# Block 0's first transposed tokens move into the tile of the forms, and its first residual runs its readings before the sums, the biases and LayerNorm's small operations

## The chip, the cores and the metric

The kernel runs on one core of a Trainium2 chip. A core has TensorE (matrix products from SBUF into PSUM), VectorE, ScalarE and GpSimd, each with a queue of its own that runs in order, and DMA queues, most of whose transfers SyncE issues. Engines wait for each other through semaphores alone. The metric is the device time of one execution in microseconds (us), the median of several runs.

In the profile PE is TensorE's matmuls, PEld its weight loads, DVE is VectorE, ACT is ScalarE, POOL is GpSimd and SP is SyncE. L701 is line 701 of the kernel before.

## What is computed

The input x has two sequences of 2048 tokens of 512 values, and each sequence has a condition vector. The condition gives six vectors (shift, scale and gate for each of two halves), and each half is a LayerNorm, a modulation and a two-layer network with a gated residual:

```python
emb = silu(t) @ ada_w + ada_b
shift_msa, scale_msa, gate_msa, shift_mlp, scale_mlp, gate_mlp = split(emb, 6)
norm  = ln(x) * (1 + scale_msa) + shift_msa
h     = gelu_exact(norm @ ssm_w1 + ssm_b1)            # 512 -> 512
x     = x + gate_msa * (h @ ssm_w2 + ssm_b2)          # 512 -> 512
norm2 = ln(x) * (1 + scale_mlp) + shift_mlp
hf    = gelu_tanh(norm2 @ ff_w1 + ff_b1)              # 512 -> 1024
x     = x + gate_mlp * (hf @ ff_w2 + ff_b2)           # 1024 -> 512
```

All values are float32.

## The kernel before

**Tiles and names.** The 4096 tokens are eight blocks of 512, each in an SBUF tile x of 128 partitions and four slots c of 512 values. Most large tiles come from one pool of eight buffers (`big`): brows, the x blocks, the weights ada_0 to ada_5 of the condition, the transposed tokens nT and the hidden values hA, hClo and hChi. A new tile takes a buffer that has been released, and its first write waits until the last reader of the old tile is done. The tile `forms`, 16 parts in all, is a constant. From block 1 on it holds sums of transposed tokens; in block 0 its first eight parts hold the hidden values hA (`hA_0`), and its other eight hold nothing that early.

**Products.** A layer is not one matrix product. Operands and results are cut in two by two, and seven products P1 to P7 are made where eight would be needed. The price is sums of operands before (three new operands per side, made by `sums_of_first` and `sums_of_second`: s0, s1, then one quarter changed in place, then s2) and sums of results after. Each product of 512 by 512 is a group of eight matmuls of 256 columns. The results of several products add up in one PSUM tile: P1, P6, P7 and P4 share the tile y, P5 and P3 the tile v, and P2 has x. After each product VectorE reads the tile (`after`), and the next product into the same tile waits for that reading. The products of block 0's and block 1's first layers and of their first residual run in the order `FIRST`, which is P1, P2, P5, P6, P7, P3, P4. P3 of a residual needs s2 of the hidden values, P5 and P6 need s0 and s1, P7 the quarter that is changed in place.

**The order is written by hand.** `hook(hooks, places, ops)` hangs operations behind products. After product P's matmuls and its reading have been issued, the operations hooked to P are issued, each to the queue of its engine. So where a hook stands decides what an engine does before what.

**The stage around the change.** For block 0 the start runs so: LayerNorm of block 0; the first halves of the modulation vectors of groups 0 and 1 (`modulation`, matmuls L279 with the weights ada_0 and ada_1); the transposes by TensorE (L898); the second halves of the same modulation; then `modulate` (L596 on ScalarE for k = 0 and 2, L598 on VectorE for k = 1 and 3), which writes nT; the sums nS of nT; the first layer (`First(0, ...)`, tiles py_hA, px_hA, pv_hA). Behind its products are hooked the rows of the gate, the folding of the gate into w2 (`fold2`: 0 to 3 are products on VectorE, 4 to 7 the four sums of w2 on GpSimd), the gated bias b2 that is added to x's slots on GpSimd (`gb2`, four operations L713, one for each slot), the first two statistics of block 1 and the modulation of group 3.

Then follows block 0's first residual (`residual("oA_0", ...)`, readings at L701). Behind its products are hooked the rest of the sums of the hidden values (`hA_sums`, tile hSA), the other two statistics of block 1, its LayerNorm scales (`scales`), its normals (`normal`, x times rstd plus nmr, L553 on ScalarE or L557 elsewhere), the modulation of group 4, the transposes of block 1 (`turned`), the first statistics of block 0's second LayerNorm, and the first three of the four sums of the weights fw1 (`fw1_sums`, GpSimd, tile fw_s; the third changes fw1 itself).

`scales` has two forms. Both begin on GpSimd with ve (L502) and the power r (L504). By default six more small operations run on GpSimd (L515 to L520); with `on_dve=True` four run on VectorE (L510 to L513).

**Loads.** SyncE issues the loads in the order of the program: x_0, ada_0 and ada_1 by halves, w1 by halves, ada_2, w2, b2, x_1, ada_3, ada_4, fw1, and, after the first modulation, ada_5, fw2 and rows of the second gate's bias.

From block 1 on the first layer of the second half is made of 26 products (`products`, L800) instead.

Of the kernel before, what the change touches and what calls it, by code (L numbers as in the profile page):

```python
# [140 lines left out]
def kernel(  # L141
# [16 lines left out]
    nc = tc.nc  # L158
# [3 lines left out]
    KD = D // P  # L162
    KH = H // P
    C = 4
# [29 lines left out]
    def big_tile(name):  # L194
        return big.tile([P, KD, D], F32, tag="big", name=name)
# [71 lines left out]
    def modulation(g0, part, half=None):  # L267


        g = g0 + part  # L270
        if not half:
            pada[g] = ps_g.tile([P, D], F32, tag="x", name=f"pada_{g}")
            mods[g0, part] = const.tile([P, KD, B], F32, tag=f"mod_{g0}_{part}", name=f"mod_{g0}_{part}")
        n = slice(0, KD) if half is None else slice(half * KD // 2, (half + 1) * KD // 2)
        pa = pada[g][:, n.start * G : n.stop * G]
        w = ada[g].rearrange("p k (n m q) -> p k m n q", n=KD, q=G)
        for k in range(KD):
            for m in range(P // G):
                nc.tensor.matmul(  # L279
                    pa[m * G : (m + 1) * G, :],  # L280
                    silu[:, k, :],
                    w[:, k, m, n],
                    start=(k == 0),
                    stop=(k == KD - 1),
                    tile_position=(0, m * G),
                    skip_group_check=True,
                )
        turned = pada[g][:, P + n.start * G : P + n.stop * G]
        bias = colsT[:, R_ADA + g * KD : R_ADA + (g + 1) * KD][:, n]

        def finish():
            nc.vector.transpose(turned, pa)
            to = mods[g0, part][:, n]
            by_n = turned.rearrange("p (n q) -> p n q", q=G)
            nc.vector.tensor_tensor(
                to, by_n[:, :, :B], bias.unsqueeze(2).to_broadcast([P, n.stop - n.start, B]), ALU.add
            )

        if half is not None:
            return finish  # L300
        finish()
# [106 lines left out]
    def weight_of_first(name, w_sb):  # L408

        K, M = w_sb.shape[1], w_sb.shape[2]  # L410
        tile_s = const.tile([P, 3, K // 2, M // 2], F32, tag=f"{name}_s", name=f"{name}_s")
        s = thirds(tile_s)
        lo, hi = w_sb[:, : K // 2, :], w_sb[:, K // 2 :, :]
        q = quarters(lo, hi, slice(0, M // 2), slice(M // 2, M))
        return first_operands(q, s), sums_of_first(q, s, nc.gpsimd), tile_s
# [58 lines left out]
    def hook(hooks, places, ops):  # L474

        for n, op in enumerate(ops):
            hooks.setdefault(places[min(n, len(places) - 1)], []).append(op)


    class Norm:  # L480
# [64 lines left out]
        def normal(self, c, eng=None, on_pe=False):  # L545

            if c == 0:
                self.nT = big_tile(f"nT{self.name}")
                self.xn = self.blocks().rearrange("p m k c q -> p m (k c q)") if on_pe else self.nT
            t = self.xn[:, c, :]  # L550
            x_c = xs[self.i][:, c, :]
            if eng is None:
                nc.scalar.activation(  # L553
                    t, x_c, AF.Identity, bias=self.nmr[:, c : c + 1], scale=self.rstd[:, c : c + 1]
                )
            else:
                eng.tensor_scalar(  # L557
                    t, x_c, self.rstd[:, c : c + 1], self.nmr[:, c : c + 1], ALU.mult, ALU.add
                )
# [127 lines left out]
    def residual(name, i, hops, wops, kdim, hooks, last=False, order=ORDER):  # L687

        xt = xs[i]
        F = D // 2  # L690
        q = {
            "11": xt[:, 0:2, :F],
            "12": xt[:, 0:2, F:],
            "21": xt[:, 2:4, :F],
            "22": xt[:, 2:4, F:],
        }
        dest = {"P1": "11", "P2": "11", "P6": "12", "P5": "22", "P7": "22", "P3": "12", "P4": "21"}

        def after(p, ps, js):
            d = q[dest[p]][:, js]  # L700
            nc.vector.tensor_tensor(d, ps[BANK[p]][:, js], d, ALU.add)  # L701
            if last and p in ("P7", "P4"):
                s = slice(2 + js.start, 2 + js.stop)
                f = slice(F, D) if p == "P7" else slice(0, F)
                nc.sync.dma_start(out=out_blk[i][:, s, f], in_=xt[:, s, f])

        parted = ("P1", "P6", "P7", "P4") if last else ()
        group(name, kdim, hops, lambda p, j, k: wops[p][:, k, :], after, hooks, parted, order)

    def biases(i, gb):  # L710

        return [
            lambda c=c: nc.gpsimd.tensor_tensor(xs[i][:, c, :], xs[i][:, c, :], gb, ALU.add)  # L713
            for c in range(C)
        ]
# [9 lines left out]

    forms = const.tile([P, 16, C, HT // C], F32, tag="forms", name="forms")

    hA_0 = forms[:, :8].rearrange("p n a r -> p (n a r)").rearrange("p (k t) -> p k t", k=KD)

    def sums_of_registers(program, reg, engs):  # L730

# [112 lines left out]
    n1 = {0: Norm(0, 1), 1: Norm(1, 1)}  # L844
# [22 lines left out]
    st = n1[0].stats()  # L867
# [59 lines left out]
    def fold2(lo, hi):  # L927
        return [lambda k=k: found["w2"][1][k]() for k in range(lo, hi)]
# [14 lines left out]
    hooks = {}  # L943
# [3 lines left out]
    st = n1[1].stats()  # L947
    hook(hooks, ("P6",), [rows_of_ssm_gate])
    gb2 = biases(0, b2_bc)
    hook(hooks, ("P3",), [ssm_gate, gb2_0] + gb2[:2] + fold2(0, 2))  # L950
    hook(hooks, ("P7",), fold2(2, 6) + gb2[2:] + fold2(6, 7))
    hook(hooks, ("P7", "P4"), st[:2])
    hook(hooks, ("P7",), [lambda: modulation(3, 0)])
    hA[0] = First(0, n1[0].ops, hooks, ("P1", "P2", "P5", "P6", "P3", "P7", "P4"), hA_0)
# [2 lines left out]
    hA_sums = hA[0].summed(nc.vector)  # L957
    run(hA_sums[:2])
    hooks = {}
    hook(hooks, ("P1",), hA_sums[2:3] + st[2:] + [n1[1].scales] + fold2(7, 8))  # L960
    hook(hooks, ("P2",), hA_sums[3:] + [lambda c=c: n1[1].normal(c, on_pe=True) for c in range(C)])
    hook(hooks, ("P6",), [lambda: modulation(3, 1)])
    hook(hooks, ("P3", "P3", "P4"), n1[1].turned())
    n2 = {0: Norm(0, 2)}
    st = n2[0].stats()
    hook(hooks, ("P3",), st[:2])
    fw1_ops, fw1_sums, fw1_s = weight_of_first("fw1", fw1_sb)
    hook(hooks, ("P2",), fw1_sums[:1])
    hook(hooks, ("P5", "P4"), fw1_sums[1:3])
    residual("oA_0", 0, hA[0], w2_ops, KD // 2, hooks, order=FIRST)  # L970

    def ff_gate():
# [12 lines left out]
    hooks = {}  # L985
# [15 lines left out]
    hA_sums = hA[1].summed(nc.vector)  # L1001
    run(hA_sums[:2])
    n1[2] = Norm(2, 1)
    st = n1[2].stats()
    hooks = {}
# [15 lines left out]
    hooks = {}  # L1021
# [26 lines left out]
    hooks = {}  # L1048
# [10 lines left out]
    hooks = {}  # L1059
# [6 lines left out]
    hooks = {}  # L1066
# [11 lines left out]
    for i in range(1, NBLK):  # L1078
        nxt, nx2, last = i + 1 < NBLK, i + 2 < NBLK, i + 1 == NBLK
        hC = Second(i)  # L1080
        hooks = {}
# [19 lines left out]
        hooks = {}  # L1101
# [16 lines left out]
        hooks = {}  # L1118
# [58 lines left out]
        hooks = {}  # L1177
# [52 lines left out]
```

## Time and profile before

| | us |
|---|---|
| median of 3 runs | 599.33 (598.78 to 599.54) |
| the profiled execution | 598.88 |
| its span, first to last instruction | 597.0 |

The profiled execution's own time is the one that its rows add up to; 1.9 us of it lie around the span.

The granted clock of TensorE is 1.00 in every stretch of this execution, so a matmul costs the same at each place: eight matmuls of 256 columns start 1.73 us after the eight before, where nothing is waited for.

The busy time of the engines by stretches of ten microseconds (us, from the profile's windows):

| stretch | DVE | ACT | POOL | DMA GB/s |
|---|---|---|---|---|
| 0 to 10 | 4.56 | 2.54 | 3.66 | 276 |
| 10 to 20 | 8.34 | 3.53 | 4.98 | 398 |
| 20 to 30 | 9.30 | 1.96 | 5.25 | 412 |
| 30 to 40 | 9.14 | 1.06 | 8.85 | 404 |
| 40 to 50 | 7.46 | 5.53 | 7.91 | 144 |
| 50 to 60 | 8.77 | 5.29 | 9.18 | 8 |
| 60 to 70 | 9.51 | 3.16 | 2.22 | 127 |
| 70 to 80 | 9.07 | 5.57 | 9.34 | 7 |
| 80 to 90 | 8.52 | 3.28 | 8.12 | 99 |

How to read it: the loads run at full speed until 40 us. VectorE is the fullest of the four in the stretch of the change. A stretched instruction (one that took longer because of another) counts as busy for its whole length.

The waits that the profile lists for TensorE's matmuls are few. In each line come the instruction that waited, what it waited for, the total in us, how often, and the longest:

```profile
PE idle L862 <- POOL ident masks.py:199: 1.3, 1, 1.3
PE py_oA L459 <- DVE x L701: 1.2, 1, 1.2
PE py_hA L459 <- ACT nT L596: 0.5, 1, 0.5
PE pt L898 <- ACT blocks L553: 0.2, 1, 0.2
```

The first belongs to the warm-up at the very start. The second is in block 0's first residual, the third at the first group of block 0's first layer.

### The profile page before, as it was taken

The numbers are of one execution on the slowest core, as the hardware profiler recorded it, in microseconds if no ns is written. First come the engines' busy times: TensorE is split into PE (matmuls) and PEld (weight loads), VectorE is DVE, ScalarE is ACT, GpSimd is POOL, SyncE is SP. The second block draws the span as 40 slices with busy tenths as digits, with TensorE's granted clock in tenths as the row PEclk, the third lists the DMA queues.
The fourth block names the chain that finished last, engine by engine and source line by source line (L and its number), as shares of the span: only waits on it lengthen the run. The fifth ranks groups of instructions, "written<-read, shape, count | busy, mean of one in ns | idle before, by whom it ended". The sixth has DMA issues, their size and how long they took to land.

```text
span 597.0 us, 8378 instructions
## 1 busy us (share of the span) xinstructions
PE 590.3 (99%) x2911; PEld 510.1 (85%) x2911; DVE 374.4 (63%) x646; ACT 219.7 (37%) x365; POOL 397.1 (67%) x467
## 2 busy tenths in 40 slices
PE   8999999999999999999999999999999999999997
PEld 4778888888888888888888888888888888888886
DVE  5978998897654375555754458653665246467642
ACT  2234347305432363233721356232553235212420
POOL 2698489999843995549968499966974596440200
PEclk9999999999999999999999999999999999999999
DMA  9990322300224003350042601321020300022001
GB/s 312 411 372 4 86 71 78 101 35 36 71 71 121 22 0 94 148 146 3 13 146 61 210 13 41 102 71 71 0 63 9 107 36 1 1 59 83 0 1 70
DMA packets 25065, 49.86 MB, mean 84 GB/s; under 512 B 4498, under 2 KB 8126, under 8 KB 24128
## 3 DMA queue, kind: packets, MB, share of 16 engines
q1 hardware_dynamic: 21984, 45.11, 22.7%
q10 hardware_dynamic: 3040, 4.22, 2.8%
q8 instruction: 23, 0.38, 0.3%
q14 instruction: 18, 0.15, 0.1%
HBM read 26.25 MB, written 8.39 MB: 58 GB/s over the span
## 4 chain that ended last, share of the span: by engine, by line
PE 96%; DVE 2%; issue 0%; ACT 0%; POOL 0%; POOLq 0%
PE py_oC L459 19%; PE px_hC L800 10%; PE pv_oC L459 9%; PE py_oA L459 9%; PE py_hA L459 9%; PE py_hC L800 8%; PE pv_hC L800 8%; PE pv_hA L459 5%; PE px_oC L459 5%; PE pv_oA L459 4%; PE py_hC L459 2%; PE px_hA L459 2%; PE px_oA L459 2%; PE pv_hC L459 1%; PE idle L862 1%; PE px_hC L459 1%
## 5 line engine op out<-in xcount | busy, mean ns | idle before, releaser
L713 POOL TENSOR_TENSOR x<-x,gb 128x512 f32<-128x512 f32 x64 | 80.3, 1286 | 8.7 <-ACT forms L670 4.7
L596 ACT ACTIVATE nT<-nT,mod,mod 128x512 f32<-128x512 f32 x54 | 39.6, 803 | 104.8 <-DMA nT<-blocks 98.0
L553 ACT ACTIVATE nT<-x,nmr,rstd 128x512 f32<-128x512 f32 x56 | 42.4, 803 | 52.6 <-POOL nmr L520 36.8
L502 POOL TENSOR_SCALAR ve<-mv 128x4 f32<-128x4 f32 x15 | 3.5, 233 | 82.2 <-DVE mv L494 81.9
L459 PE MATMUL py_oC<-fw,hClo 128*128 128x256 f32 x256 | 57.9, 379 | 0.0
L459 PEld LDWEIGHTS py_oC<-fw,hClo 128*128 128x128 f32 x256 | 48.6, 190 | 6.6
L701 DVE TENSOR_TENSOR x<-py_oC,x 128x512 f32<-128x512 f32 (+1 forms) x36 | 22.6, 629 | 42.6 <-PE py_oC L459 42.6
L493 DVE BATCH_NORM_STATS2 st<-x 128x6 f32<-128x512 f32 x64 | 43.4, 678 | 5.2 <-DMA x<-in_x_dram 5.0
L379 POOL TENSOR_TENSOR hSC<-hClo,hChi 128x512 f32<-128x512 f32 (+1 forms) x17 | 20.1, 1188 | 39.6 <-ACT hChi L795 29.2
L800 PE MATMUL py_hC<-forms,fw 128*128 128x256 f32 x168 | 40.8, 379 | 0.0
L817 DVE TENSOR_TENSOR hClo<-hClo,py_hC 128x512 f32<-128x512 f32 x42 | 28.4, 681 | 16.9 <-ACT hClo L814 10.3
L564 DVE STREAM_TRANSPOSE blocks<-nT 128x512 f32<-128x512 f32 x56 | 37.8, 693 | 1.5 <-ACT nT L553 1.1
L738 POOL TENSOR_TENSOR forms<-forms 128x256 f32<-128x256 f32 x48 | 35.6, 742 | 2.8
L800 PEld LDWEIGHTS py_hC<-forms,fw 128*128 128x128 f32 x168 | 31.8, 190 | 4.4
L817 DVE TENSOR_TENSOR hChi<-hChi,pv_hC 128x512 f32<-128x512 f32 x35 | 23.3, 683 | 17.1 <-PE pv_hC L800 17.1
L701 DVE TENSOR_TENSOR x<-py_oA,x 128x512 f32<-128x512 f32 x32 | 22.0, 688 | 19.2 <-PE py_oA L459 18.7
L459 PE MATMUL py_hA<-nT,w 128*128 128x256 f32 x128 | 30.4, 381 | 0.5 <-ACT nT L596 0.5
L795 ACT ACTIVATE hClo<-hClo,colsT 128x256 f32<-128x256 f32 x56 | 25.4, 500 | 10.8 <-DVE hClo L817 10.7
L459 PE MATMUL py_oC<-fw_s,hSC 128*128 128x256 f32 x128 | 28.9, 379 | 0.0
L459 PE MATMUL pv_oC<-fw,hSC 128*128 128x256 f32 x128 | 28.9, 379 | 0.0
L459 PE MATMUL px_oC<-fw,hChi 128*128 128x256 f32 x128 | 28.9, 379 | 0.0
L459 PE MATMUL pv_oC<-fw_s,hSC 128*128 128x256 f32 x128 | 28.9, 379 | 0.0
(227 smaller groups left out, 1428.4 us busy)
## 6 DMA issues: line engine op xcount, KB each, us to landing
nT<-blocks SPq DMA_DIRECT2D x168, 64.0 KB
out_dram<-x SPq DMA_DIRECT2D x15, 512.0 KB
x<-in_x_dram SPq DMA_DIRECT2D x7, 1024.0 KB
fw<-in_L_cond_ff_w_dram SPq DMA_DIRECT2D x3, 2048.0 KB
ada<-in_L_cond_ada_w_dram SPq DMA_DIRECT2D x4, 1024.0 KB
nT<-blocks ACTq DMA_DIRECT2D x56, 64.0 KB
ada<-in_L_cond_ada_w_dram SPq DMA_DIRECT2D x4, 512.0 KB
w<-in_L_cond_ssm_w_dram SPq DMA_DIRECT2D x2, 1024.0 KB
```

Source lines behind the costliest of these rows:

```text
L379: eng.tensor_tensor(out[:, r], a[:, r], b[:, r], f)
L459: nc.tensor.matmul(ps[b][j * apart][:, j, :], lhs(p, j, k), rhs(p, j, k), start=(fresh and j * (not apart) == 0 and k == 0), stop=(p in (" ...
L493: nc.vector.bn_stats(st, xs[self.i][:, c, :])
L553: nc.scalar.activation(t, x_c, AF.Identity, bias=self.nmr[:, c : c + 1], scale=self.rstd[:, c : c + 1])
L564: nc.vector.transpose(self.bl[:, :, :, c, :].rearrange("p m k q -> p k m q"), self.nT[:, c, :].rearrange("p (k m q) -> p k m q", k=KD, m=C),)
L596: nc.scalar.activation(dst, src, AF.Identity, bias=shift, scale=scale)
L701: nc.vector.tensor_tensor(d, ps[BANK[p]][:, js], d, ALU.add)
L713: lambda c=c: nc.gpsimd.tensor_tensor(xs[i][:, c, :], xs[i][:, c, :], gb, ALU.add)
L738: eng.tensor_tensor(reg[d], reg[a], reg[b], ALU.add if f == "+" else ALU.subtract)
L795: nc.scalar.activation(h, h, AF.Gelu_apprx_tanh, bias=fb1T[:, m : m + 1])
L800: nc.tensor.matmul(ps[b][:, j, :], fa[ra][:, j * P : (j + 1) * P], fb[rb].rearrange("p a (c q) -> p c a q", q=Q), start=(fresh and j == 0) ...
L817: nc.vector.tensor_tensor(dest(d), dest(d), ps[b], op)
```

## The change

1. nT of block 0's first LayerNorm no longer takes a buffer of the pool; it is the second half of `forms`. The later tiles of the pool take other buffers than before.
2. In block 0's first residual the third new operand of the hidden values (`hA_sums[3:]`) and block 1's scales and normals are hooked to P6, so that the readings of P2, P5 and P6 come before them in VectorE's queue.
3. The scales of block 1 are made on VectorE (after ve and r on GpSimd): four small operations more on VectorE, six fewer on GpSimd. The normal of slot 3 is made by VectorE in place of ScalarE.
4. The bias of slots 2 and 3 (`gb2[2:]`) moves from block 0's first layer to P7 of the residual. In GpSimd's queue the sums of w2 close up. Then come ve, r, the first sum of fw1, the two biases, and the second and third sum of fw1. Since P7's reading writes the same slots of x before, the biases now follow that reading, and P4's reading follows the biases.
5. The first sums of fw1 are hooked to P6, P3 and P4.

No other queue changes its order; SyncE's is the same.

```diff
         def normal(self, c, eng=None, on_pe=False):

             if c == 0:
-                self.nT = big_tile(f"nT{self.name}")
+                self.nT = nT_0 if self.name == "1_0" else big_tile(f"nT{self.name}")
...
-    hA_0 = forms[:, :8].rearrange("p n a r -> p (n a r)").rearrange("p (k t) -> p k t", k=KD)
+    hA_0, nT_0 = [
+        forms[:, n : n + 8].rearrange("p n a r -> p (n a r)").rearrange("p (k t) -> p k t", k=KD)
+        for n in (0, 8)
+    ]
...
     hook(hooks, ("P3",), [ssm_gate, gb2_0] + gb2[:2] + fold2(0, 2))
-    hook(hooks, ("P7",), fold2(2, 6) + gb2[2:] + fold2(6, 7))
+    hook(hooks, ("P7",), fold2(2, 7))
...
-    hook(hooks, ("P1",), hA_sums[2:3] + st[2:] + [n1[1].scales] + fold2(7, 8))
-    hook(hooks, ("P2",), hA_sums[3:] + [lambda c=c: n1[1].normal(c, on_pe=True) for c in range(C)])
-    hook(hooks, ("P6",), [lambda: modulation(3, 1)])
+    hook(hooks, ("P1",), hA_sums[2:3] + st[2:] + fold2(7, 8))
+    hook(hooks, ("P6",), [lambda: n1[1].scales(on_dve=True)] + hA_sums[3:] + [lambda: modulation(3, 1)])
+    hook(hooks, ("P6",), [lambda c=c: n1[1].normal(c, nc.vector if c == 3 else None, on_pe=True) for c in range(C)])
     hook(hooks, ("P3", "P3", "P4"), n1[1].turned())
...
-    hook(hooks, ("P2",), fw1_sums[:1])
-    hook(hooks, ("P5", "P4"), fw1_sums[1:3])
+    hook(hooks, ("P6",), fw1_sums[:1])
+    hook(hooks, ("P7",), gb2[2:])
+    hook(hooks, ("P3", "P4"), fw1_sums[1:3])
     residual("oA_0", 0, hA[0], w2_ops, KD // 2, hooks, order=FIRST)
```

## The prediction

> **What bounds the kernel.** I read the page first, then the chain of waits, then the timelines of TensorE, VectorE and GpSimd between 10 and 85 us, where every instruction that the change touches stands.
>
> ```profile
> PE 590.3 (99%) x2911; PEld 510.1 (85%) x2911; DVE 374.4 (63%) x646; ACT 219.7 (37%) x365; POOL 397.1 (67%) x467
> PE 96%; DVE 2%; issue 0%; ACT 0%; POOL 0%; POOLq 0%
> ```
>
> TensorE is the bound: 96% of the chain that ended last is its own work. Only the start of a group of eight matmuls can move. Groups follow each other every 1.73 us from 84 to 545 us, so what is won or lost before 84 us stays to the end. The one large hole in that stretch is here:
>
> ```profile
> 36.73 1.08 PE L279 MATMUL pada<-ada,silu 128*32 128x128 f32 x32
> 39.03 1.97 PE L459 MATMUL py_oA<-w,forms 128*128 128x256 f32 x8 [1.22 <-DVE x L701]
> ```
>
> P7 of block 0's second product could start at 37.65 (the last matmul of the modulation starts at 37.54) and starts at 39.03. It adds into the PSUM tile of P6, so it waits for VectorE's reading of P6, which is late because VectorE is busy without a gap from 25 to 39.3 us:
>
> ```profile
> 36.33 0.18 DVE L494 BATCH_NORM_AGGREGATE mv<-st 128x2 f32<-128x6 f32 x1
> 36.43 0.66 DVE L701 TENSOR_TENSOR x<-px_oA,x 128x512 f32<-128x512 f32 x1
> 37.00 0.68 DVE L379 TENSOR_TENSOR hSA<-forms,hSA 128x512 f32<-128x512 f32 x1
> 37.60 0.68 DVE L701 TENSOR_TENSOR x<-pv_oA,x 128x512 f32<-128x512 f32 x1
> 38.20 0.68 DVE L701 TENSOR_TENSOR x<-py_oA,x 128x512 f32<-128x512 f32 x1
> ```
>
> 38.20 + 0.68 + 0.15 for the semaphore is 39.03. The fourth view is GpSimd's queue beside two VectorE rows:
>
> ```profile
> 36.91 1.03 POOL L504 TENSOR_TENSOR r<-ve,minus_half 128x4 f32<-128x4 f32 x1
> 40.87 2.37 POOL L379 TENSOR_TENSOR fw_s<-fw 128x1024 f32<-128x1024 f32 x1
> 45.64 2.35 POOL L379 TENSOR_TENSOR fw<-fw 128x1024 f32<-128x1024 f32 x1
> 58.66 2.36 POOL L379 TENSOR_TENSOR fw_s<-fw,fw_s 128x1024 f32<-128x1024 f32 x1
> ```
> ```profile
> 46.91 1.63 DVE L379 TENSOR_TENSOR nS<-nT 128x512 f32<-128x512 f32 x1
> 59.25 2.32 DVE L379 TENSOR_TENSOR hSA<-hA 128x512 f32<-128x512 f32 x1 [0.70 <-ACT hA L670]
> 61.61 0.69 DVE L379 TENSOR_TENSOR hSA<-hSA,hA 128x512 f32<-128x512 f32 x1
> ```
>
> The same VectorE addition takes 0.69 us alone and 2.32 us beside GpSimd's 58.66 to 61.02: it ends 0.55 after that instruction, as does the one at 46.91 (47.99 + 0.55 = 48.54). Additions with a PSUM input, such as the three L701 above, never show this.
>
> **Part 1: block 0's first nT in forms.** Before, it takes the buffer of ada_0, so its first writes (ScalarE L596 and VectorE L598, both at 13.26) wait for the second modulation batch that reads ada_0. Their own inputs are there earlier: the modulation columns at 11.91, the transposes of k = 0 and 1 at 11.95 and 12.17. In forms they start at 12.0 and 12.2, and TensorE's first group at about 13.5, when the modulation batch ends, in place of 14.09: 0.6 early. It doesn't last. The modulation of group 3 (26.89) needs ada_3, the last of the first 8.65 MB on the load queue; the windows show 2.76, 3.98 and 4.12 MB in the first three 10 us, so the queue delivers it at about 24.6, and the last of its sixteen completions is at 26.75. Before, TensorE was ready at 26.7 and started at 26.89; now it is ready at 26.1 and starts at 26.89. Worth to TensorE: 0. VectorE keeps some of it, since its queue has no other wait until 33 us: I take 0.4, bounded by 0 and 0.7 (its additions at 15 to 22 us fall differently on GpSimd's four w_s sums there, each a wait of up to 1 us).
>
> **Part 2: readings first.** The third sum of hSA goes behind the readings of P5 and P6: 0.60 (the pitch of these rows). Two of the four bias additions leave GpSimd at 30.95 to 34.34; the w2 sums that take their place end sooner, so the VectorE rows at 31.57 and 33.74 (1.64 and 1.16, each stretched by a GpSimd instruction) cost about 0.4 less. P6's reading ends at 38.88 - 0.4 - 0.4 - 0.6 = 37.5, and P7 starts at 37.7 in place of 39.03: **1.3 us gained at this point.**
>
> **Part 3: what now stands in front of P3.** P3 needs that third sum, and VectorE now runs four small operations (L510 to L513) before it. They need r from GpSimd. The statistics end at 36.51 - 0.8 = 35.7, so r ends at 37.94 - 0.8 = 37.15; and the next instruction in GpSimd's queue is now fw_s<-fw, 2.37 us, from 37.2 to 39.6 (its weights are there: their last completion is at 34.49). The first small operation, r times ve, comes to VectorE's head at about 37.5, in the middle of it. Here a rule of the Trainium skill speaks against the change: "SBUF — State Buffer", section "Who interferes with whom", says that a VectorE instruction with two SBUF inputs contends with a GpSimd instruction that reads SBUF, that the first to start keeps the port pair for its whole length, and that the other fully blocks. It doesn't ask for the size. The rows above show it for 512 columns; for 4 columns they show only the reverse (GpSimd's 128x4 product at 51.96 takes 0.64 in place of 0.20 beside a VectorE addition). In one point the row differs: the pow (36.91 to 37.94) reads SBUF and did not stretch the hSA sum at 37.00 (0.68), so I let r block nothing. By the rule: small operations from 39.6 to 40.2 (0.75 for four, as the same four take at 527.34 in block 7), the sum to 40.85, P3 at 41.0, against 40.83 before. By their bare durations: 37.5 + 0.8 + 0.6 = 38.9, P3 at 39.4 right behind P7. I take the rule: **all of the 1.3 is gone, 0.2 lost**, ends -1.3 and +0.5.
>
> The rest of this queue is covered: ScalarE's three normals run 40.25 to 42.45, VectorE's one (0.55, at 10.17 two of them take 1.00) ends near 42.1, the transposes are due at 42.75. P7's reading ends at 42.65, P4 is due at 43.6. The bias of slots 2 and 3 ends at 45.2, P4's reading is due at 45.5: cover 0.3.
>
> **Part 4: GpSimd's queue ends later.** Before: fw sums 40.87 to 47.99, then idle 2.26. Now the two bias additions stand between the first and second fw sum and wait for P7's reading: 42.7 to 45.2, then 2.35 and 2.35: to about 49.5 to 50.0, some 1.5 to 2 us later. In that time VectorE wants block 1's two nS sums (46.91 and 48.65 before; only the first was stretched). The second now waits for fw<-fw and ends between 50.0 and 51.0, in place of 49.34, by who takes the port first at 46.9. Behind it in VectorE's queue stand a statistic (0.8) and the reading of P1 (0.6), which P6 of block 1's first product waits for (same PSUM tile): 51.55 to 52.55 in place of 51.21. Where it is 51.55, the reading of P6 is still 0.5 late and P7 starts 0.5 late, and each new wait of TensorE adds about 0.1 (after the one at 39.03 the second matmul is 0.29 behind the first, not 0.22). **Part 4 costs 0.6 to 1.4; I take 0.9**, with the 0.2 of part 3: +1.1. Later statistics and normals of block 0 move with it; the DMA turn behind them has 1.7 us of cover (nT done at 70.14, TensorE at 71.90), and nothing is left that could win it back.
>
> **Sum.** The profiled execution took 598.88 (span 597.0): 598.88 + 1.1 = 600.0. The median of the runs, 599.33, lies 0.45 above the profiled one, so the time to compare is **600.4**, 0.18% slower. What can be told from no change here is about 0.2%, 1.2 us; the forecast lies at that edge.
>
> **Rivals and chances.**
> - **Likeliest, 0.50:** as summed, +0.6 to +1.7, 599.9 to 601.0; half of it beyond 1.2.
> - **A. The port costs more, 0.17:** fw<-fw takes the port before the first nS sum as well, so both sums wait (two stretches, 1.1 + 1.7), and the hSA addition at 59.25 meets a later fw_s. For it: that addition already loses 1.63. Against: TensorE waits only where a reading is later than its group's 1.73. +1.7 to +2.8, about 601.5.
> - **B. Not slower, 0.18:** operations of four columns pass beside GpSimd. The place is L510; the price is 2.1 us, and it decides once fw_s starts before the last reading ends. For it: at 8.39 the 128x2 product takes 0.15 beside GpSimd's ve; against it: GpSimd's own 128x4 operations are held. Then the third sum alone waits (39.6 + 0.55), P3 starts at 40.3, 0.5 early, and part 4, with GpSimd 0.7 less late, takes 0.5 to 0.9: 599.3 to 599.8.
> - **C. Faster, 0.15:** GpSimd's late queue meets nothing that TensorE waits for and L510 isn't held; part 2 stays: 599.33 - 1.3 = 598.0. For it: VectorE has gaps of 1.71 and 1.03 at 39.3 and 41.7. Against it: both rows at 46.91 and 59.25.
>
> That the move into forms brings the 0.6 us to the end would need ada_3 before 26.1; nothing speaks for it. Faster 0.13 (most of C), within 0.2% 0.44 (half of the likeliest, B, a little of C), slower 0.43 (the other half and A). The range 598.6 to 602.0 leaves out most of C and the tail of A; the likeliest alone is 599.9 to 601.0.
>
> **What would show it.** Right: TensorE's first group near 13.5 and the modulation again at 26.9; P7 near 37.7; a VectorE L510 row of about 2 us that ends with GpSimd's fw_s; TensorE waiting about 1.5 us at P3; an nS row stretched beyond 2 us near 48. Wrong: L510 at 0.16 us beside fw_s, or P3 directly behind P7. The forecast falls if GpSimd's fw sums end before VectorE comes to block 1's nS sums.

## The result, and the profile after

| | before | after |
|---|---|---|
| median of 13 runs each | 599.14 us (598.56 to 599.60) | 600.27 us (599.99 to 600.86) |
| span of the profiled execution | 597.0 us | 598.2 us |

The ratio is 1.0019, with a 95% interval of 1.0011 to 1.0028: slower by about 1.1 us. The forecast was 600.4. TensorE's busy time is 590.3 us in both kernels and its granted clock is 1.00 in every stretch of ten microseconds around the change, so the difference is waiting.

The list of TensorE's waits of the changed kernel (what waited, for what, total in us, how often, longest), and the chain's shares by engine:

```profile
PE pv_oA L459 <- DVE hSA L379: 1.1, 1, 1.1
PE pada L279 <- DMA ada<-in_L_cond_ada_w_dram: 0.6, 1, 0.6
PE py_hA L459 <- DVE hA L653: 0.5, 1, 0.5
...
PE py_oA L459 <- DVE x L701: 0.3, 1, 0.3
```
```profile
PE 91%; DVE 5%; DMA 2%; issue 1%; POOL 1%; ACT 0%; ACTq 0%; DVEq 0%; POOLq 0%
```

The wait of 1.2 us for the reading of P6 is gone. In its place stand a wait of P3 for the third hidden sum, one for ada_3, one for a reading of block 1, and a shorter one for a reading in block 1's residual. TensorE's own share of the chain fell from 96% to 91%. Where the waits lie, from TensorE's timeline (start, duration, line, tiles; in brackets the idle time before and what ended it):

```profile
36.63 1.08 PE L279 MATMUL pada<-ada,silu 128*32 128x128 f32 x32
37.84 1.96 PE L459 MATMUL py_oA<-w,forms 128*128 128x256 f32 x8
40.95 1.99 PE L459 MATMUL pv_oA<-w,hSA 128*128 128x256 f32 x8 [1.15 <-DVE hSA L379]
...
52.08 1.99 PE L459 MATMUL py_hA<-nS,w_s 128*128 128x256 f32 x8 [0.48 <-DVE hA L653]
```

P7 starts at 37.84 in place of 39.03. P3 then waits 1.15 us and starts at 40.95, before at 40.83. VectorE and GpSimd in the same stretch and in block 1's first layer, and last the row of the kernel before for the second nS sum:

```profile
37.01 0.68 DVE L701 TENSOR_TENSOR x<-py_oA,x 128x512 f32<-128x512 f32 x1
37.61 2.09 DVE L510 TENSOR_TENSOR e<-r,ve 128x4 f32<-128x4 f32 x1
...
40.21 0.68 DVE L379 TENSOR_TENSOR hSA<-forms,hSA 128x512 f32<-128x512 f32 x1
...
47.21 0.66 DVE L379 TENSOR_TENSOR nS<-nT 128x512 f32<-128x512 f32 x1
47.97 2.65 DVE L379 TENSOR_TENSOR nS<-nT,nS 128x512 f32<-128x512 f32 x1
```
```profile
37.33 2.35 POOL L379 TENSOR_TENSOR fw_s<-fw 128x1024 f32<-128x1024 f32 x1
42.47 2.50 POOL L713 TENSOR_TENSOR x<-x,gb 128x512 f32<-128x512 f32 x2 [2.79 <-DVE x L701]
...
47.24 2.83 POOL L379 TENSOR_TENSOR fw<-fw 128x1024 f32<-128x1024 f32 x1
```
```profile
48.65 0.69 DVE L379 TENSOR_TENSOR nS<-nT,nS 128x512 f32<-128x512 f32 x1
```

A product of four columns takes 2.09 us and ends at 39.70, with GpSimd's fw_s (37.33 + 2.35 = 39.68). Ten microseconds later the second nS sum takes 2.65 us and ends 0.55 behind GpSimd's fw<-fw (47.24 + 2.83 = 50.07). The last of the three fw sums ends 2.1 us later than before (47.99): the bias additions in front of it wait 2.79 us for P7's reading, and fw<-fw itself takes 2.83 us in place of 2.35, because the first nS sum is in front of it.

### The profile page after: what moved, and what is told of

Read it like the earlier page. It is cut to its first block, busy times and chain, and to the rows that moved or that the text cites. A ratio compares the mean times of both kernels' runs of the same rounds, so it can differ in the third digit from the quotient of the medians.

```text
span 598.2 us, 8375 instructions
## 1 busy us (share of the span) xinstructions
PE 590.3 (99%) x2911; PEld 510.0 (85%) x2911; DVE 378.4 (63%) x651; ACT 218.9 (37%) x364; POOL 396.2 (66%) x461
## 4 chain that ended last, share of the span: by engine, by line
PE 91%; DVE 5%; DMA 2%; issue 1%; POOL 1%; ACT 0%; ACTq 0%; DVEq 0%; POOLq 0%
PE py_oC L459 18%; PE px_hC L803 10%; PE pv_oC L459 9%; PE py_oA L459 8%; PE py_hC L803 8%; PE pv_hC L803 8%; PE py_hA L459 8%; PE px_oC L459 5%; PE pv_oA L459 4%; PE pv_hA L459 4%; PE py_hC L459 2%; PE px_hA L459 2%; PE px_oA L459 2%; DMA w<-in_L_cond_ssm_w_dram 1%; PE pv_hC L459 1%; DVE hSA L379 1%
## 5 line engine op out<-in xcount | busy, mean ns | idle before, releaser
L701 DVE TENSOR_TENSOR x<-py_oC,x 128x512 f32<-128x512 f32 (+1 forms) x36 | 22.6, 630 | 42.6 <-PE py_oC L459 42.6
L564 DVE STREAM_TRANSPOSE blocks<-nT 128x512 f32<-128x512 f32 x56 | 37.7, 693 | 1.8 <-ACT nT L553 1.4
L701 DVE TENSOR_TENSOR x<-py_oA,x 128x512 f32<-128x512 f32 x32 | 22.0, 688 | 17.6 <-PE py_oA L459 17.0
L459 PE MATMUL py_oC<-fw_s,hChi 128*128 128x256 f32 x128 | 28.9, 379 | 0.0
```

Of the source, the lines that this page charges most:

```text
L459: nc.tensor.matmul(ps[b][j * apart][:, j, :], lhs(p, j, k), rhs(p, j, k), start=(fresh and j * (not apart) == 0 and k == 0), stop=(p in (" ...
L564: nc.vector.transpose(self.bl[:, :, :, c, :].rearrange("p m k q -> p k m q"), self.nT[:, c, :].rearrange("p (k m q) -> p k m q", k=KD, m=C),)
```

## The experiments

All are read in one table: how much later (+) or earlier (-) than in the kernel before TensorE starts a group, in us, from the timelines. The heads give the start in the kernel before. "Block 1, P6" is in its first layer; "hC" is block 0's second layer. The last columns are the medians, with that of the kernel before on the same chip, and the ratio with its interval.

| kernel | P7 39.03 | P3 40.83 | P4 43.43 | block 1, P6 51.21 | hC P1 71.90 | hC P6 75.36 | 93.30 | time (before) | ratio |
|---|---|---|---|---|---|---|---|---|---|
| changed | -1.19 | +0.12 | +0.22 | +0.87 | +1.32 | +1.32 | +1.17 | 600.27 (599.14) | 1.0019 [1.0011, 1.0028] |
| e1 | -0.52 | -0.52 | -0.52 | -0.52 | -0.50 | -0.50 | -0.59 | 598.47 (598.92) | 0.9993 [0.9985, 1.0001] |
| e2 | -0.71 | -0.71 | +0.20 | +0.20 | +0.34 | +0.51 | +0.55 | 599.36 (598.92) | 1.0007 [0.9999, 1.0016] |
| e3 | -1.09 | -1.09 | -0.44 | +1.31 | +1.72 | +1.81 | +1.86 | 600.53 (598.92) | 1.0029 [1.0018, 1.0039] |
| e4 | -1.12 | -1.12 | -1.12 | +1.48 | +2.79 | +3.82 | +3.86 | 602.62 (598.92) | 1.0053 [1.0040, 1.0066] |
| e5 | -1.16 | +5.01 | +7.69 | +7.96 | +7.54 | +8.80 | +8.84 | 607.12 (599.01) | 1.0131 [1.0115, 1.0146] |
| e6 | -0.06 | +1.24 | +1.35 | +2.00 | +2.44 | +2.44 | +2.41 | 600.74 (599.01) | 1.0027 [1.0016, 1.0038] |
| e7 | -1.18 | +0.13 | +0.23 | +0.23 | +1.39 | +1.39 | +0.76 | 599.71 (599.01) | 1.0012 [1.0005, 1.0018] |
| e8 | -1.08 | -1.08 | -0.76 | -0.63 | -1.05 | -0.03 | +0.01 | 599.04 (599.01) | 1.0002 [0.9994, 1.0010] |
| e9 | -1.17 | -1.17 | -0.85 | -0.73 | -1.15 | -1.05 | -0.53 | 598.45 (598.91) | 0.9989 [0.9982, 0.9995] |
| e10 | -1.10 | -1.10 | -0.79 | -0.68 | -1.10 | -0.53 | -0.48 | 598.36 (598.91) | 0.9992 [0.9986, 0.9999] |

### e1: part 1 alone

On the kernel before:

```diff
-                self.nT = big_tile(f"nT{self.name}")
+                self.nT = nT_0 if self.name == "1_0" else big_tile(f"nT{self.name}")
...
+    hA_0, nT_0 = [
```

> Part 1 alone: the kernel before with block 0's first nT in the tile of the forms, nothing else. Theory of the prediction (the move is pinned by ada_3's load for TensorE, but VectorE keeps its 0.6 us): first group of block 0 near 13.5, modulation of group 3 again at about 26.8, P7 of the residual near 38.4 in place of 39.03, since the whole VectorE queue in front of its reading is 0.6 earlier; 0.5 to 0.8 us faster than before at the end. Rival 1 (the 0.6 is eaten by the collisions with GpSimd's sums on the way or by ada_3, nothing of it reaches P7): within 0.2 us of before. Rival 2 (the rotation of the pool's buffers costs something: later tiles wait for other readers): slower than before, with a new wait of TensorE or of a first write of a large tile behind 50 us.

The first group starts at 13.59, the modulation of group 3 at 26.82 after 0.59 us of waiting for ada_3: the gain does not pass through TensorE. It passes through VectorE, whose rows are 0.52 earlier up to the reading of P6; P7 starts at 38.51, and this stays to the end. The median is 0.45 us below that of the kernel before; the interval just includes 1. The collisions with GpSimd that were feared on the way cost nothing more.

### e2: the readings first, alone

On the kernel before:

```diff
-    hook(hooks, ("P2",), hA_sums[3:] + [lambda c=c: n1[1].normal(c, on_pe=True) for c in range(C)])
-    hook(hooks, ("P6",), [lambda: modulation(3, 1)])
+    hook(hooks, ("P2",), [lambda c=c: n1[1].normal(c, on_pe=True) for c in range(C)])
+    hook(hooks, ("P6",), hA_sums[3:] + [lambda: modulation(3, 1)])
```

> Part 2 alone: the kernel before with only the third sum of hSA moved behind the readings of P5 and P6; nT, the scales, the biases and the sums of fw1 as before. Theory: P7 at about 38.4 (one 0.60 earlier than 39.03), the third sum ends near 39.2, before P3 is due, so P3 starts right behind P7; the block 1 transposes are held by its normals (they end near 42.4 as before), so 0.3 to 0.6 us of this stay: faster by 0.2 to 0.6. Rival (the order of the readings is itself what costs in the changed kernel, since P3's sum now comes after three readings): P3 waits for hSA and the time is that of before or up to 0.5 us slower.

P7 and P3 are 0.71 early, as expected, and the rival's wait at P3 is not there. Yet nothing stays: P4 is 0.20 late. VectorE's and GpSimd's timelines of e2:

```profile
38.09 0.68 DVE L379 TENSOR_TENSOR hSA<-forms,hSA 128x512 f32<-128x512 f32 x1
```
```profile
38.19 0.63 POOL L516 TENSOR_TENSOR e<-e,ve 128x4 f32<-128x4 f32 x1
```

The sum that was moved now runs beside GpSimd's four-column product, which takes 0.63 in place of 0.20 (before, at 38.30). The scales end 0.34 later, so ScalarE's four normals end at 42.98 in place of 42.64, and the transposes of block 1 before P4 wait for the last one. The expectation took the normals' end as given; it depends on where the sum runs. It also promised too much: P4 starts 0.65 us after the last normal here, so with the old end, 42.64, it would have come at about 43.29, only some 0.14 early (an estimate from these rows). So the order of the readings is worth next to nothing unless the normals come earlier too.

### e3: the changed kernel with the scales on GpSimd

```diff
-    hook(hooks, ("P6",), [lambda: n1[1].scales(on_dve=True)] + hA_sums[3:] + [lambda: modulation(3, 1)])
+    hook(hooks, ("P6",), [lambda: n1[1].scales()] + hA_sums[3:] + [lambda: modulation(3, 1)])
```

> The changed kernel with block 1's scales back on GpSimd: six small operations there, none on VectorE. fw_s then starts behind them, near 38.7. Theory (the four-column L510 was held by GpSimd's fw_s): no L510 row, the third sum of hSA at 37.6 right behind the readings with 0.68 us, P3 right behind P7 near 39.3, 1.5 us earlier than in the changed kernel; GpSimd's sums end about 1.4 us later still, near 51.5 if nothing else moves, so the stretch of block 1's second nS sum stays or grows: at 52 us 0 to 0.9 later than before, the end 0.2 to 1.2 us slower than before and up to 0.9 faster than the changed kernel. Rival 1 (the lateness at the end comes from L510's stall alone): 1 us or more faster than before. Rival 2 (the stall is not the port; the small operations only waited for r): P3 not earlier than 40.5.

Without the small operations P3 follows P7 directly: 1.09 early. Rivals 1 and 2 both fall: the stall at P3 goes, and the end is later, not earlier. It is later than expected because a stall was overlooked:

```profile
39.67 2.58 DVE L557 TENSOR_SCALAR blocks<-x,rstd,nmr 128x512 f32<-128x512 f32 x1 [0.84 <-POOL nmr L520]
```
```profile
39.60 2.36 POOL L379 TENSOR_TENSOR fw_s<-fw 128x1024 f32<-128x1024 f32 x1
```

VectorE's normal of slot 3, 0.54 us in the changed kernel, is now the one that meets fw_s, and takes 2.58. P7's reading stands behind it, so the biases start at 42.92, and block 1's nS sums take 1.28 and 2.65.

### e4: the changed kernel, no GpSimd sum at L510

```diff
-    hook(hooks, ("P6",), fw1_sums[:1])
-    hook(hooks, ("P7",), gb2[2:])
+    hook(hooks, ("P7",), gb2[2:] + fw1_sums[:1])
```

> The changed kernel with the first sum of fw1 behind the two bias additions in GpSimd's queue; the scales stay on VectorE. Now no GpSimd sum is in flight when L510 comes. Theory (port): L510 takes about 0.16 us at 37.6, the third sum ends near 39, P3 near 39.3 right behind P7. In return the biases run from about 40.5 to 43 and the three sums of fw1 end near 50.1 or later, as late as in the changed kernel, while TensorE and so block 1's nS sums come 1.5 us earlier and meet two of them: both nS sums stretched, block 1's P6 of the first product waits more than 1.5 us, and the end is 0.8 to 2.2 us slower than before, no better than the changed kernel. Rival 1 (L510 itself is what costs at the end): about 1 us faster than before. Rival 2 (L510 waits for r or for its own queue, not for the port): L510 stays at 2 us.

VectorE's timeline, and TensorE's windows (stretch, its length, busy time and matmuls, granted clock, DMA share, GB/s):

```profile
37.68 0.15 DVE L510 TENSOR_TENSOR e<-r,ve 128x4 f32<-128x4 f32 x1
...
45.87 2.61 DVE L379 TENSOR_TENSOR nS<-nT 128x512 f32<-128x512 f32 x1
48.58 2.65 DVE L379 TENSOR_TENSOR nS<-nT,nS 128x512 f32<-128x512 f32 x1
```
```profile
50.00:52.00 2.00, 0.53 (x3) 1.00 0.00 0
52.00:54.00 2.00, 1.30 (x3) 0.65 0.00 0
54.00:56.00 2.00, 2.00 (x6) 0.50 0.00 0
```

The same instruction, with r as early as in the changed kernel, takes 0.15 us when no GpSimd sum is in flight: the 2.09 us were the wait for GpSimd's sum, and P3 is 1.12 early. The bill comes at block 1's nS sums, both held for 2.6 us, and P6 there waits 2.17 us. The end is worse than expected for a reason that no theory had: at the end of that wait TensorE's clock fell to half, and the group after it took 3.62 us in place of 1.89. Three of the five runs have this time (602.6 to 602.9) and a mean clock of 0.996 to 0.997, two do not (600.9, clock 1.00): without it the end is 1.9 to 2.0 us later than before, inside the range expected. The last 1.0 us up to +3.8 in the profiled execution is the wait at 75 us that e8 is about.

### e5: the changed kernel with the biases in their old place

```diff
-    hook(hooks, ("P7",), fold2(2, 7))
+    hook(hooks, ("P7",), fold2(2, 6) + gb2[2:] + fold2(6, 7))
...
-    hook(hooks, ("P7",), gb2[2:])
```

> The changed kernel with the bias of slots 2 and 3 back in block 0's first layer, where the kernel before has it; all else as changed. GpSimd's three sums of fw1 then follow r without the two bias additions between them. The first two have nothing to wait for; the third waits for nothing either. Theory a (the first to start keeps the port for its own instruction alone, so VectorE gets in between two sums): L510 is 2 us or less, P3 at most 0.5 later than before, GpSimd's sums end near 45, before block 1's nS sums, so these take 0.69 us each and the end is within 0.6 us of before. Theory b (GpSimd's next instruction starts at the end of the one before, so VectorE waits through the row of sums): L510 about 6.5 to 7 us, from 37.6 to 44.5, P3 near 45.6, and the end 4 to 5 us slower than before. Rival (the stall at L510 doesn't depend on what GpSimd does): a row of 2 us and the changed kernel's 1.2 us slower.

VectorE's four operations, and GpSimd's sums beside them:

```profile
38.17 2.30 DVE L510 TENSOR_TENSOR e<-r,ve 128x4 f32<-128x4 f32 x1 [0.44 <-POOL r L504]
40.50 0.16 DVE L511 SCALAR_TENSOR_TENSOR e<-e,r 128x4 f32<-128x4 f32 x1
40.70 2.19 DVE L512 SCALAR_TENSOR_TENSOR rstd<-e,r 128x4 f32<-128x4 f32 x1
42.92 2.26 DVE L513 SCALAR_TENSOR_TENSOR nmr<-mv,rstd 128x4 f32<-128x4 f32 x1
```
```profile
38.11 2.34 POOL L379 TENSOR_TENSOR fw_s<-fw 128x1024 f32<-128x1024 f32 x1
40.53 2.34 POOL L379 TENSOR_TENSOR fw_s<-fw_s,fw 128x1024 f32<-128x1024 f32 x1
42.83 2.33 POOL L379 TENSOR_TENSOR fw<-fw 128x1024 f32<-128x1024 f32 x1
```

Theory a has the mechanism right and the number wrong; theory b has P3 about right (45.6, measured 45.84) and the mechanism wrong. The port is given back after each GpSimd instruction: L510 ends with the first sum (40.47, the sum at 40.45), and L511 slips in before the next. But L512 and L513 are instructions of their own, and each ends with a sum again (42.89 and 45.18, the sums at 42.87 and 45.16): four operations worth 0.75 us take 7.0. TensorE is idle for 6.0 us, and its clock is at 0.50 from 46 to 50 us, which turns the 5.0 us at P3 into 7.7 at P4, and makes the end 8.1 us late where b said 4 to 5. That the biases now stand between the first and the second fw sum, and wait there for P7's reading, is what keeps the changed kernel at one stall.

### e6: the changed kernel without the move into forms

```diff
-                self.nT = nT_0 if self.name == "1_0" else big_tile(f"nT{self.name}")
+                self.nT = big_tile(f"nT{self.name}")
```

> The changed kernel with block 0's first nT back in the pool's buffer; all else as changed. Theory: part 1 is worth its 0.6 us to VectorE's queue also here, so P7 is 0.6 later than in the changed kernel (38.4), L510 begins at 38.2 and still ends with GpSimd's fw_s, which begins 0.6 later too; everything behind moves by about 0.6: 0.5 to 0.8 us slower than the changed kernel, 1.7 to 2.0 slower than before. Rival 1 (the order of GpSimd and VectorE at the second nS sum turns out otherwise, so the 0.6 is lost in a collision): as the changed kernel within 0.2. Rival 2 (the move into forms is what makes the changed kernel slow): faster than the changed kernel.

P7 is 1.13 later than in the changed kernel in the profiled executions. Not all of it is the move's: VectorE's gated bias (L925 before, L928 here) starts at 25.08 in the kernel before, at 25.61 in e6 and at 24.48 in the changed kernel. Up to there e6 does what the kernel before does, so 0.53 us is the late start of this one execution (it is the slowest of its seven runs), and 0.60 is the move's. L510 again takes 2.09 and the second nS 2.65. The excess over the kernel before is 1.73 by the medians, 1.13 in the changed kernel: 0.6 for part 1, though the two intervals overlap. Both rivals fall.

### e7: the changed kernel, fw<-fw away from block 1's nS sums

```diff
-    hook(hooks, ("P3", "P4"), fw1_sums[1:3])
+    hook(hooks, ("P3",), fw1_sums[1:2])
...
-    hook(hooks, ("P1",), hA_sums[2:3] + fw1_sums[3:])
+    hook(hooks, ("P1",), hA_sums[2:3] + fw1_sums[2:])
```

> The changed kernel with the third sum of fw1 (the one that changes fw1 in place, 2.35 us or more on GpSimd) moved from block 0's residual to block 1's, directly in front of the fourth. Theory (part 4: the second nS sum of block 1 waits for this instruction): both nS sums take about 0.7 us, TensorE's P6 of block 1's first product starts 0.2 later than before in place of 0.87, and stays so to 59 us. Behind that two GpSimd sums stand beside the hSA sums of block 1's residual in place of one, so P6 there waits for both: about 0.9 to 1.3 later than before from 63 us, the end 0.7 to 1.3 slower than before. Rival (the 0.65 at 52 us has another cause, such as the readings' order or the statistics): TensorE's P6 at 52 us is as in the changed kernel, 0.6 or more later than before.

The nS sums take 0.66 and 0.69, and from P4's +0.23 nothing grows until 61 us: the 0.65 that the changed kernel loses at 51 us is this one GpSimd instruction. The collision moves into block 1's residual (hSA rows of 1.45 and 2.72), where it costs 1.16; 0.63 of it comes back between 76 and 85 us, where the kernel before itself waits for VectorE. The end is at +0.76.

### e8, e9, e10: can both kernels be beaten?

e8 takes e1 and e2 together on the kernel before, gives ScalarE one normal less, and puts block 1's nS sums behind its statistics:

```diff
+    hook(hooks, ("P2",), [lambda c=c: n1[1].normal(c, on_pe=True) for c in range(3)])
+    hook(hooks, ("P6",), hA_sums[3:] + [lambda: modulation(3, 1)] + [lambda: n1[1].normal(3, nc.vector, on_pe=True)])
...
-    run(st[2:3] + n1_sums[:2] + st[3:])
+    run(st[2:] + n1_sums[:2])
```

> The parts that showed a gain, put together on the kernel before: nT of block 0 in forms, the third sum of hSA behind the readings, the scales on GpSimd, the biases and sums of fw1 in their old places; VectorE makes the normal of slot 3, so that ScalarE's three end earlier; and block 1's two nS sums stand behind its last two statistics, by which time GpSimd's third fw1 sum is about to end. Theory: P7 near 37.9 (1.1 early), P3 behind it, the transposes not held, one nS sum of about 1.1 to 1.3 us, TensorE 1.0 early at 52 us and 1.0 to 1.4 early at 72 us: 0.8 to 1.4 us faster than before. Rival 1 (VectorE's normal is held by GpSimd's w2 or fw1 sum, as a row of 2.58 us in the run with the scales on GpSimd suggests, and the reading of P7 with it): 0.3 to 0.8 faster. Rival 2 (a wait behind 72 us takes it all back): within 0.3 of before.

The lead of 1.05 us reaches 73 us and is gone at 75.36: rival 2. VectorE's timeline of e8, and ScalarE's copy of the second gate in e8, in the kernel before and in e1:

```profile
70.90 0.69 DVE L983 TENSOR_TENSOR gb<-pgate,gb 128x512 f32<-128x512 f32 x1 [2.27 <-ACT pgate L367]
...
74.50 0.68 DVE L653 TENSOR_TENSOR hClo<-py_hC,colsT 128x512 f32<-128x512 f32 x1
```
```profile
70.28 0.59 ACT L367 COPY pgate<-gsb 128x512 f32<-128x512 f32 x1 [0.28 <-DMA gsb<-gates]
```
```profile
70.28 0.59 ACT L367 COPY pgate<-gsb 128x512 f32<-128x512 f32 x1
```
```profile
69.69 0.57 ACT L367 COPY pgate<-gsb 128x512 f32<-128x512 f32 x1
```

The second gate is written to memory and loaded again, and in e8 it comes no earlier than before. VectorE waits 2.27 us for it with the readings of P3 and P4 behind, so hC's P1 is read at 74.50 and P6 waits for that. The gate's time is not fixed: e1, with a lead of 0.5 us, has it 0.59 us earlier and keeps its lead. SyncE starts the four stores at 63.13 in the kernel before, at 62.61 in e1 and at 62.49 in e8, but issuing them takes 2.66, 2.65 and 3.64 us, so e8's load follows as late as before (67.23, before 67.17, e1 66.36). In e4, e5, e9 and e10 the stores take 3.4 to 3.8 us too; why is not shown, so what ends e8's lead is known only as far as these stores. e9 and e10 are e8 with the second gate's work in other places: e9 puts the readings in front of it and spreads its products, e10 puts all of it behind P4's reading:

```diff
-    hook(hooks, ("P7",), [gb5_0] + n2_sums[1:] + [lambda c=c: n1[2].normal(c) for c in range(C)] + gb5)
-    hook(hooks, ("P7", "P3", "P4"), fold5(0, 3))
+    hook(hooks, ("P7",), n2_sums[1:] + [lambda c=c: n1[2].normal(c) for c in range(C)])
+    hook(hooks, ("P4",), [gb5_0] + gb5)
+    hook(hooks, ("P4",), fold5(0, 1))
...
-    hook(hooks, ("P6", "P5", "P7", "P3", "P4"), fold5(3, 8))
+    hook(hooks, ("P6", "P5", "P7", "P3", "P3", "P4", "P4"), fold5(1, 8))
```

This is e9; e10 has `fold5(0, 3)` behind P4 and leaves the last line as it was.

> The combined kernel (e8), whose lead of 1.05 us at 71.9 is gone at 75.36, with the second gate's VectorE work in block 1's residual moved: the gated bias (L983) and the first product of fw2 go from P7 behind P4's reading, the next two products into the first half layer of block 0, spread behind P6 to P4. Theory (the lead ends at the second gate, pgate at 70.28 as in the kernel before; VectorE's queue waits there with the readings of P3 and P4 behind it, and the reading of P1 of the next layer, which TensorE waits for, comes at 74.50): P3's and P4's readings are now taken when their products end, P1's reading at about 73, TensorE's P6 at about 74.3 in place of 75.33, so the lead of 1 us passes 75 us. Of this VectorE, which is full between 78 and 86, may take back 0.1 to 0.6 by the two products that were moved there: 0.4 to 1.0 us faster than before. Rival (the lead is held by something else at 75 us, such as the sums nS of block 0's second layer on GpSimd, or is taken back wholly by VectorE behind 78): within 0.2 us of before.

> As e9, but all three products stand behind P4's reading, directly ahead of the reading of P1. Theory: the readings of P3 and P4 are free, but the reading of P1 now stands behind the gated bias and three products, at about 74.1 in place of 74.50, so TensorE's P6 starts about 0.4 earlier than in e8: 0.3 to 0.6 us faster than before. Rival (the order in VectorE's queue there doesn't matter): as e8, within 0.2 us of before.

In e9 the gate is again not early (copied at 70.44), but hC's P1 is read at 72.75 and a lead of 1.05 passes 75 us. VectorE, with the two products more, takes half of it back at 88 us (-1.07 to -0.53). e10 loses the same half at 75 us, because the products stand ahead of P1's reading. By the medians both end about 0.5 us faster than the kernel before on the same chip, which the changed kernel misses by 1.13; their intervals lie wholly below 1, that of e10 barely.

## Why the prediction was right

**Part 1** (TensorE 0, VectorE 0.4): the mechanism is as told. The first group starts at 13.52, the modulation at 26.79 after 0.6 us for ada_3. VectorE keeps 0.59 (P1's reading at 32.55 in place of 33.14), so the term was 0.2 too small; e1 (0.5) and e6 (0.6) show its worth.

**Part 2** (0.60 + 0.4 + 0.4, P7 at 37.7): P7 came at 37.84. One of the three terms was wrong. "Some 0.4 from fewer collisions" did not occur: the rows at 30.99 and 33.15 take 1.64 and 1.16, to the hundredth as before. The w2 sums that moved into the biases' place hold VectorE as long as the biases did. The two mis-sizings, 0.2 and 0.4, have opposite signs and leave 0.2; that P7 came so near is partly luck.

**Part 3** (L510 blocked, P3 at 41.0): 2.09 us, P3 at 40.95, and +0.22 once TensorE runs again (predicted 0.2). Here the prediction chose a rule over the bare duration, with rows of 512 columns alone behind it; e4 (0.15 us) and e5 (a stall for each sum) show that it holds for four. Rival B is refuted. One reading was thin: the three L701 rows shown for PSUM inputs stand beside no GpSimd sum; those of the kernel before at 41.03 and 42.76 do, beside fw_s (40.87 to 43.24), and take 0.69, so the reading holds.

**Part 4** (0.6 to 1.4, taken 0.9): fw<-fw ends at 50.07, the second nS at 50.62, block 1's P6 starts at 52.08, each inside or at the edge of what was worked out. The sizes: 0.65 at P6 (e7 takes exactly this away); 0.16 more up to 54.05, of which 0.10 is the restart after the wait (P6's second matmul is 0.32 us behind its first, in place of 0.22) and the rest P6's late reading; then 0.28 in block 1's residual that the likeliest case did not have: the first hSA sum starts 1.17 later than before, where TensorE is 1.04 late, and takes 2.47 in place of 2.32 beside fw_s. Behind 73 us 0.15 comes back, which "nothing is left that could win it back" excluded wrongly. 0.65 + 0.16 + 0.28 - 0.15 = 0.94, so that the sum met 0.9 owes something to two terms that it did not have.

**Sum**: 0.22 + 0.94 = 1.16, forecast 1.1; the spans differ by 1.2 and the medians by 1.13. (The forecast of 600.4 stood on the three runs' median of 599.33; on 599.14 the same sum gives 600.2.) The mechanism is the one predicted, the closeness of the total is in part luck. Rival A saw the residual's collision but as part of a double one; the first nS sum slipped in before fw<-fw and took 0.66. It did so by 0.03 us (47.21 against 47.24); in e3 and e4 it met a sum of fw1 and took 1.28 and 2.61. Rival C needed L510 free and GpSimd's late queue to meet nothing; e4 shows that the first alone is no gain at all.

## What to carry to other kernels

A reorder that brings one reading forward also brings everything behind it into another neighbour's time: list for each moved instruction of VectorE which GpSimd instruction is in flight when it will run, and the reverse. A short instruction is held as long as a long one if the other engine has the port, so operations of 0.16 us belong beside no long GpSimd sum, and a chain of them pays once for each sum. A lead must be followed to the next thing that may not move with it (here a load at 26.8 and, in e8, a gate at 70.3): what stands behind that in the waiting engine's queue loses the lead, what stands ahead of it keeps it (e9).

## What the runs showed of the hardware that was not expected

- VectorE's `TENSOR_SCALAR` from SBUF to SBUF (L557), with one tensor input, is held by GpSimd's sums like an addition of two: 2.58 us in e3, 0.54 in the changed kernel. The Trainium skill, "SBUF — State Buffer", section "Who interferes with whom", counts `tensor_scalar` among the operations that can enter a mode with both ports and so contend; the trace agrees, and the prediction had no such term.
- GpSimd's power L504, 1.04 us long, reads SBUF too and did not hold VectorE's additions: VectorE's nT<-nT takes 0.68 us at 51.95 beside the one at 51.85.
- The hold works on GpSimd as well: fw<-fw takes 2.83 us when a VectorE sum is in front of it, 2.35 otherwise, and a four-column product 0.63 in place of 0.20.
- TensorE's clock fell to one half after it had been idle 2.2 us in e4, and after 6.0 us in e5 (profiled executions); by the mean clocks it did so in three of five runs of e4 and in all four of e5 (0.993 to 0.994). After 1.5 us in e3 it never did in seven (1.00). The Trainium skill, "TensorE: Matmul & The Clock Gate", section "Part 1: The HAM clock gate", gives one idle window of about 3.4 us, which runs free of the kernel, as what halves the clock; here 2.2 us were enough at times, and the fall cost 1.7 us in e4.
